# Sparse attention in steps of three instead of two, with transposed keys one trio ahead

## The chip, the cores and the metric

The program runs on one core of a Trainium2 chip. The metric is the device time of one execution in microseconds. Engines are named as in the profile: PE is TensorE's matmul, PEld its weight load, DVE VectorE, ACT ScalarE, POOL GpSimd and SP SyncE, which here only issues transfers.

## The reference

One layer of graph attention and one layer of experts, each with a residual, on 4096 nodes of 512 features. All arithmetic is float32.

```python
def _L0_gnn_ref(x, adj, Wks, Wqs, Wvs, Wo):       # 8 heads of 64
    adj = max(adj, eye)
    q, k, v = (einsum('nd,hdk->hnk', x, W) for W in (Wqs, Wks, Wvs))
    scores = einsum('hqk,hmk->hqm', q, k) * 64 ** -0.5
    scores = scores + 0.01 * eye - 1e16 * (1 - adj)
    return einsum('hqm,hmk,hko->qo', softmax(scores), v, Wo)

def _L0_ffn_ref(x, Wg, bg, W1, b1, W2, b2):       # 8 experts, the best 2 of each row
    w, idx = top_k(x @ Wg + bg, 2)
    y = gelu(x @ W1[e] + b1[e]) @ W2[e] + b2[e]   # for the two chosen e
    return sum(softmax(w) * y)

x = x + _L0_gnn_ref(layernorm(x), adj, ...)
x = x + _L0_ffn_ref(layernorm(x), ...)
```

The adjacency is sparse, with more edges among the first nodes: an edge has a probability that falls with the numbers of both nodes.

## The kernel before

The program has three stages. The first (0 to about 467 us) normalises x, makes keys, values and queries, turns the adjacency into bit masks, and builds for each tile of 128 queries a list of the nodes that some query of the tile is joined to. A row of `kv_d` holds for one node its 512 keys, its values with a column of ones, and its mask words: `KVW` words of four bytes, 4,640 bytes in all. The third stage (from about 1543 us) runs the experts on rows sorted by expert. The stage between, attention, is where the change lies.

**Steps.** Each of the 32 tiles of queries (`i`) is worked through in steps (L639 to L650). The first step of a tile is "own": the 128 nodes of the tile itself. A "both" step has 128 gathered nodes that are scored against all 128 queries. A "split" step has twice 128 gathered nodes, of which one set is scored against the first 64 queries, the other against the last 64. `ROOM` (L31) says how many there are: with `(3, 2, 3)` a tile has own, both, split, both, split, split. There are 270 steps in all, 115 both, 123 split and 32 own, that need 361 gathered sets of 128 rows and 32 of a tile's own.

**Duos.** Up to two consecutive steps of a tile make a duo (L654). The loop L1100 to L1118 has one slot `n` for each duo, and in it, in program order: `scores` of duo n + 1, `values` of duo n, the ends of tiles and new transfers, the jobs that were laid on slot n (`later`), and `turn` of duo n + 3. Engines run their instructions in this order; semaphores tie them where data does.

- `turn` (L711): PE transposes the keys of the step, four or eight 128 x 128 transposes, into a PSUM buffer of `bank`; ACT copies it to `kT` (L720); DVE spreads the mask words to `t` (L730).
- `scores` (L744): PE multiplies kT with the queries, 8 products of 64 x 128 for an own or both step, 32 of 64 x 64 for a split one (L755; each float32 product shows as two matmuls in the trace). ACT takes the exponential into `pr` (L762), DVE multiplies by the mask (L766, L768).
- `values` (L774): PE multiplies pr with the values of the ring's row and adds up in `o` (L783).

**Buffers.** `ps_r` has three PSUM buffers of two banks each; `bank()` (L661) hands them out in turn for scores, transposes and all jobs. `ps_o` has the last two banks. In SBUF, `step` has four buffers of kT, four of pr and six of t. `ring` is one large tile of 24 rows (`RING`); each row takes one gather.

**Transfers.** `issue` (L1053) puts the gathers of duos up to n + 5 (`AHEAD`) into the queues. A gather (L691) is an indirect DMA issued by POOL; a tile's own rows and its queries come through SP. A gather waits until the values of the step that held its row 24 rows earlier are done. When all gathers are issued, `load_weights` (L1075) brings the experts' weights into parts of the ring that fall free: `PARTS` = 7 of the eight parts lie over the ring, the eighth goes to memory that is freed when attention ends (L1116).

**Ends of tiles.** After a tile's last duo, `end_of` (L798) divides by the sums and lays jobs on later slots: transposing (`flip_o`, n + 1), the projection with Wo (`project`, L823, n + 2) and the residual. After every fourth tile `route` (L850) lays the routing of four tiles on the slots after: `root`, `norm` (ACT, L885), `flip`, `gate`, `rank`, `place`, `number_places`, `pick`, `weigh`, `finish`, and eight `scatter`s (L1010) that POOL writes with indirect DMAs to `xs_d`, two in each of four slots. The last four tiles are routed as groups of two, one and one.

Of the kernel before, what the change touches and what calls it, by code (L numbers as in the profile page):

```python
# [9 lines left out]
F32 = mybir.dt.float32  # L10
BF16 = mybir.dt.bfloat16
I32 = mybir.dt.int32
U16 = mybir.dt.uint16
# [7 lines left out]
P = 128  # L21
# [54 lines left out]
def _fast(ctx, tc, dram, flag, x, adj, Wks, Wqs, Wvs, Wo, Wg, bg, W1, b1, W2, b2, out):  # L76
    nc = tc.nc
    N, D = x.shape
    H, _, KD = Wks.shape
# [8 lines left out]
    NW = P // 16  # L88
# [231 lines left out]
    with ExitStack() as s1:  # L320
# [198 lines left out]
        def job(n, f, *args):  # L519
            jobs.setdefault(n, []).append(lambda: f(*args))  # L520

        begins = [0]
        for i in range(NT):
            begins.append(begins[-1] + (2 * DC if i < TPB else 3 * DC))
            s = begins[i]
# [7 lines left out]
        for h in range(NHC):  # L533
            s = 5 + 5 * h
# [57 lines left out]
        for i in range(NT):  # L592
            b, t = divmod(i, TPB)
# [28 lines left out]
    xs_ = {}  # L622
    scatters = []

    RING, PARTS = 24, 7
    SW = E * HID
    ringp = ctx.enter_context(tc.tile_pool(name="ring", bufs=1))
    ring = ringp.tile([P, PARTS * SW], I32, name="ring")
    with ExitStack() as s2:
# [3 lines left out]
        mid = s2.enter_context(tc.tile_pool(name="mid", bufs=1, side="right"))  # L633
        s3 = ExitStack()
        qp = s3.enter_context(tc.tile_pool(name="qp", bufs=1))
        step = s3.enter_context(tc.tile_pool(name="step", bufs=4))


        steps = []  # L639
# [11 lines left out]

        duos = []  # L654
        for i in range(NT):
            own = [n for n, st in enumerate(steps) if st["i"] == i]
            duos += [own[k : k + 2] for k in range(0, len(own), 2)]

        S = len(duos)

        def bank(name, shape):  # L661

            t = ps_r.tile([P, 2, 512], F32, tag="r", name=name)
            n = 1
            for k in shape:
                n *= k
            v = t.rearrange("p b f -> p (b f)")[:, :n]
            if len(shape) == 2:
                v = v.rearrange("p (a b) -> p a b", b=shape[1])
            elif len(shape) == 3:  # L670
                v = v.rearrange("p (a b c) -> p a b c", b=shape[1], c=shape[2])
            return v
# [5 lines left out]
        def at(n, job):  # L678
            later.setdefault(n, []).append(job)
# [22 lines left out]
        def load_q(i):  # L702
            qs[i] = qp.tile([P, NP, P], F32, tag="q", bufs=3, name=f"q_{i}")
            nc.sync.dma_start(out=qs[i], in_=q_d[:, :, ts(i, P)])
# [6 lines left out]
        def turn(s):  # L711
            st = steps[s]
            i = st["i"]
            nk = len(st["kv"])
            pk = bank(f"pkT_{s}", [2 * NP, P])
            for x, g in enumerate(st["kv"]):
                for p in range(NP):
                    nc.tensor.transpose(pk[:, x * NP + p, :], g[:, ts(p, P)], ident)  # L718
            kT = step.tile([P, 2 * NP, P], F32, tag="kT", name=f"kT_{s}")
            nc.scalar.copy(kT[:, : nk * NP], pk[:, : nk * NP])  # L720
            st["kT"] = [kT[:, x * NP : (x + 1) * NP] for x in range(nk)]
            t = step.tile([P, NW, 16], U16, tag="t", bufs=6, name=f"t_{s}")
            if st["kind"] == "own":
                words = [own_words[:, i, :]]
            else:
                words = [wv[:, i * NW : (i + 1) * NW] for wv in st["wv"]]
            nw = NW // len(words)
            for x, wv in enumerate(words):
                w = slice(x * nw, (x + 1) * nw)
                nc.vector.tensor_tensor(  # L730
                    t[:, w], wv[:, w].unsqueeze(2).to_broadcast([P, nw, 16]), bits[:, w],
                    op=ALU.bitwise_and,
                )
            st["t"] = t.rearrange("p w k -> p (w k)")
            if st["kind"] == "own":
                m = step.tile([P, P], F32, tag="m", bufs=2, name=f"m_{s}")
                nc.vector.scalar_tensor_tensor(
                    m, st["t"], 0.0, eye, op0=ALU.is_gt, op1=ALU.max
                )
                st["m"] = m  # L740
# [3 lines left out]
        def scores(s):  # L744
            st = steps[s]
            q, parts = qs[st["i"]], st["kT"]
            nq = P // len(parts)
            ps = bank(f"ps_{s}", [2, HD])

            nk = P if len(parts) == 1 else HALF  # L750
            for x, kT in enumerate(parts):
                for p in range(NP):
                    for r in range(2):
                        for c in range(0, P, nk):
                            nc.tensor.matmul(  # L755
                                ps[c : c + nk, r, p * P + x * nq : p * P + (x + 1) * nq],
                                kT[r * KD : (r + 1) * KD, p, c : c + nk],
                                q[r * KD : (r + 1) * KD, p, x * nq : (x + 1) * nq],
                                start=True, stop=True,
                            )  # L760
            pr = step.tile([P, H, P], F32, tag="pr", bufs=4, name=f"pr_{s}")
            nc.scalar.activation(  # L762
                pr.rearrange("p h q -> p (h q)"), ps.rearrange("p r f -> p (r f)"), AF.Exp
            )
            if st["kind"] == "own":
                nc.vector.tensor_mul(pr, pr, st["m"].unsqueeze(1).to_broadcast([P, H, P]))  # L766
            else:
                nc.vector.scalar_tensor_tensor(  # L768
                    pr, st["t"].unsqueeze(1).to_broadcast([P, H, P]), 0.0, pr,
                    op0=ALU.is_gt, op1=ALU.mult,  # L770
                )
            st["pr"] = pr
# [77 lines left out]
        def route(g, n):  # L850
# [159 lines left out]
            def scatter(k, j):  # L1010
                nc.gpsimd.memset(tick, 0.0)
                s = nc.gpsimd.indirect_dma_start(  # L1012
                    out=xs_d,
                    out_offset=bass.IndirectOffsetOnAxis(
                        ap=hold["slot"][:, j, k : k + 1], axis=0
                    ),
                    in_=xs_[m[k]], in_offset=None,
                )
                for t in scatters:
                    tc.declare_no_dep(s.ins, t.ins, reason="other rows")  # L1020
                scatters.append(s)
# [18 lines left out]
            n += 4  # L1040
            for k in range(G):
                for j in range(2):
                    at(n + k, lambda k=k, j=j: scatter(k, j))

        AHEAD = 5
        tick = small.tile([1, 1], F32, bufs=1, name="tick")
        wo = mid.tile([P, NP, D], F32, name="wo")
        nc.scalar.dma_start(
# [2 lines left out]
        issued = 0  # L1051

        def issue(upto, n):  # L1053
            nonlocal issued, rows_
            while issued < min(upto, S):
                sts = [steps[s] for s in duos[issued]]
                need = sum(max(1, len(st["at"])) for st in sts)
                if any(behind[(rows_ + k) % RING] > n for k in range(need)):
                    return
                for s in duos[issued]:  # L1060
                    st = steps[s]
                    if st["k"] == 0:
                        load_q(st["i"])
                    st["to"] = []
                    for x in range(max(1, len(st["at"]))):
                        k = rows_ % RING
                        behind[k] = issued
                        rows_ += 1
                        st["to"].append(ring[:, k * KVW : (k + 1) * KVW])
                        gather(s, x)  # L1070
                issued += 1
# [3 lines left out]
        def load_weights(n):  # L1075

            for k in range(PARTS):
                over_ = range(k * SW // KVW, min(RING, ((k + 1) * SW - 1) // KVW + 1))
                if issued == S and wparts[k] is None and all(behind[r] <= n for r in over_):
                    load_part(k, ring[:, k * SW : (k + 1) * SW].bitcast(F32))  # L1080
# [5 lines left out]
                nc.sync.dma_start(out=v[:, e], in_=from_[e, ts(c, P), :])  # L1086
            wparts[k] = v

        def duo(f, n):
            if n < S:  # L1090
                for s in duos[n]:
                    f(s)

        issue(AHEAD, -1)
        duo(turn, 0)
        duo(turn, 1)
        duo(scores, 0)
        duo(turn, 2)
        n = 0
        while n < S or any(k >= n for k in later):  # L1100
            duo(scores, n + 1)
            duo(values, n)
            if n < S:
                end = steps[duos[n][-1]]
                if end["last"]:
                    end_of(end["i"], n)
                    load_xi(end["i"])
                issue(n + 1 + AHEAD, n)
                load_weights(n)
            for job in later.pop(n, []):  # L1110
                job()
            duo(turn, n + 3)
            if n == S:
                s3.close()
                wff = ctx.enter_context(tc.tile_pool(name="wff", bufs=1))
                for k in range(PARTS, DC + HC):  # L1116
                    load_part(k, wff.tile([P, SW], F32, name=f"w_{k}"))
            n += 1  # L1118
# [730 lines left out]
```

## Time and profile before

| what | us |
|---|---|
| median of 3 runs (2100.89 to 2114.70) | 2109.29 |
| profiled execution | 2102.14 |
| its span, first to last instruction | 2100.4 |
| stretch 467 to 1489 (attention): PE busy | 945.3 of 1022 |
| same stretch: DVE, ACT, POOL busy | 531.5, 524.0, 450.7 |
| stretch 1489 to 1543 (routing ends): PE busy | 19.5 of 54 |

A row of a timeline is start, duration, engine, line, operation, what is written and read, and how often; a bracket tells how long the engine had been idle and what ended that. A row of waits is engine and line, what it waited for, the sum in us, how often and the longest. "issue" stands for idle time in which the engine waited for no semaphore that the profile shows. A matmul's end is modelled in the profile, so distances are taken from start to start.

### The profile page before, as it was taken

What the parts mean: (1) busy time and instruction counts of PE and PEld (TensorE: products, weight loads), DVE (VectorE), ACT (ScalarE), POOL (GpSimd) and SP (SyncE); (2) the same over time, 40 slices, a digit from 0 to 9 for tenths busy, and PEclk for the clock granted to TensorE, in tenths of its full rate; (3) what the DMA queues carried; (4) which work ended last, traced back from release to release, by engine and by line L of the source; (5) the groups of instructions that cost most, each with busy time, mean ns of one, the idle gap of its engine ahead of it and who ended that gap; (6) DMA issues with size and microseconds to landing.
All of it is one profiled execution on the core that took longest, in us unless ns stands there. A gap on an engine that the chain in (4) does not pass through costs nothing. (4 is left out here: it accounts for less than half of the span.)

```text
span 2100.4 us, 59242 instructions
## 1 busy us (share of the span) xinstructions
PE 1953.5 (93%) x25393; PEld 1302.2 (62%) x25393; DVE 952.8 (45%) x2470; ACT 794.9 (38%) x1161; POOL 603.9 (29%) x725
## 2 busy tenths in 40 slices
PE   8899999999998988998989998889579999999996
PEld 4344444448887877877878787778434444444443
DVE  3455556525544554555555554555613232332322
ACT  3233233316554544545545554445212222222221
POOL 2000000025354445354362726341312212222121
PEclk9999999999999999999999999999779999999998
DMA  9877877249787759788595959677834344433432
GB/s 371 261 248 249 260 253 249 81 179 387 239 280 252 261 202 358 237 292 291 194 376 170 366 184 359 222 276 243 306 116 70 68 71 67 70 68 69 70 66 43
DMA packets 181278, 442.30 MB, mean 211 GB/s; under 512 B 28176, under 2 KB 44560, under 8 KB 180880
## 3 DMA queue, kind: packets, MB, share of 16 engines
q0 software_dynamic: 67712, 251.55, 37.7%
q1 hardware_dynamic: 89136, 154.17, 22.7%
q10 hardware_dynamic: 24160, 32.68, 4.4%
q8 instruction: 205, 3.36, 0.6%
q14 instruction: 65, 0.53, 0.1%
HBM read 364.92 MB, written 73.42 MB: 209 GB/s over the span
## 5 line engine op out<-in xcount | busy, mean ns | idle before, releaser
L691 POOL DMA_INDIRECT ring<-kv_d,idx x361 | 396.5, 1098 | 836.6 <-ACT l L298 438.0
L768 DVE SCALAR_TENSOR_TENSOR pr<-t,pr 128x1024 f32<-128x1024 uint16 x238 | 285.1, 1228 | 265.7 <-ACT pr L762 265.7
L755 PE MATMUL ps<-q,kT 64*64 64x64 f32 (+1 forms) x10224 | 306.5, 237 | 27.5 <-issue 19.8
L783 PE MATMUL o<-ring,pr 128*64 128x65 f32 x8640 | 295.0, 225 | 33.2 <-issue 33.0
L720 ACT COPY kT<-pkT 128x512 f32<-128x512 f32 (+1 forms) x270 | 198.6, 783 | 324.6 <-PE pkT L718 315.7
L755 PEld LDWEIGHTS ps<-q,kT 64*64 64x64 f32 (+1 forms) x10224 | 273.0, 148 | 61.9 <-issue 40.6
L783 PEld LDWEIGHTS o<-ring,pr 128*64 128x64 f32 x8640 | 271.7, 139 | 49.3 <-issue 33.6
L762 ACT ACTIVATE pr<-ps 128x1024 f32<-128x1024 f32 x270 | 270.9, 1026 | 58.2 <-PE ps L755 53.3
L1227 PE MATMUL ph<-ring,xT 128*128 x552 | 251.6, 599 | 0.7 <-ACT xT L1217 0.7
L1265 POOL DMA_INDIRECT out_dram<-y,r x69 | 107.4, 1557 | 448.6 <-ACT y L1264 443.9
L718 PE MATMUL pkT<-ident,ring 128*128 128x128 f32 x1572 | 204.6, 279 | 13.4 <-ACT kT L720 6.5
L718 PEld LDWEIGHTS pkT<-ident,ring 128*128 128x128 f32 x1572 | 176.5, 143 | 39.3 <-issue 26.9
L1251 PE MATMUL py_e<-ring,hT 128*128 x414 | 189.2, 593 | 1.6 <-ACT hT L1245 1.6
L1227 PEld LDWEIGHTS ph<-ring,xT 128*128 128x128 f32 x552 | 100.6, 192 | 101.8 <-issue 100.1
L1264 ACT ACTIVATE y<-y,wt 128x512 f32<-128x512 f32 x69 | 49.8, 721 | 246.3 <-DVE y L1263 246.3
L1232 DVE COPY h<-ph 128x512 f32<-128x512 f32 x69 | 47.7, 692 | 200.7 <-PE ph L1227 200.7
L1263 DVE TENSOR_TENSOR y<-py_e,bb 128x512 f32<-128x512 f32 x69 | 47.7, 692 | 194.5 <-PE py_e L1251 194.5
L599 PE MATMUL pv<-wv,xT 128*128 128x512 f32 x256 | 132.5, 613 | 0.0
L599 PE MATMUL pk<-wk,xT 128*128 128x512 f32 x256 | 128.9, 615 | 0.7 <-ACT xT L394 0.7
L584 PE MATMUL pq<-xT,wq 128*128 128x512 f32 x256 | 125.9, 607 | 0.0
L1012 POOL DMA_INDIRECT xs_d<-x,slot_i x64 | 69.4, 1085 | 195.0 <-DVE t L730 89.2
L823 PE MATMUL py<-wo,oT 128*128 128x512 f32 x256 | 122.6, 623 | 0.0
(257 smaller groups left out, 1833.6 us busy)
## 6 DMA issues: line engine op xcount, KB each, us to landing
adj<-in_adj_dram SPq DMA_DIRECT2D x64, 1024.0 KB, 5.7
r<-xs_d SPq DMA_DIRECT2D x69, 258.0 KB, 2.7
kv_d<-kvr ACTq DMA_DIRECT2D x32, 516.0 KB, 5.8
ring<-kv_d SPq DMA_DIRECT2D x32, 516.0 KB, 6.8
ring<-in_L_ffn_W_dram SPq DMA_DIRECT2D x56, 256.0 KB, 5.3
xt<-in_x_dram SPq DMA_DIRECT2D x32, 256.0 KB, 6.1
q_d<-qT ACTq DMA_DIRECT2D x32, 256.0 KB, 2.7
q<-q_d SPq DMA_DIRECT2D x32, 256.0 KB, 5.6
```

The lines of the kernel that those rows point to most:

```text
L584: nc.tensor.matmul(pq, w["q"][:, c, ts(p, P)], xTs[b][:, c, :], start=(c == 0), stop=(c == DC - 1),)
L599: nc.tensor.matmul(pk, xTs[b][:, c, ts(t, P)], w[n][:, c, :], start=(c == 0), stop=(c == DC - 1),)
L691: nc.gpsimd.indirect_dma_start(out=g, out_offset=None, in_=kv_d, in_offset=bass.IndirectOffsetOnAxis(ap=idx[i // GL][:, i % GL, a : a + 1] ...
L718: nc.tensor.transpose(pk[:, x * NP + p, :], g[:, ts(p, P)], ident)
L720: nc.scalar.copy(kT[:, : nk * NP], pk[:, : nk * NP])
L755: nc.tensor.matmul(ps[c : c + nk, r, p * P + x * nq : p * P + (x + 1) * nq], kT[r * KD : (r + 1) * KD, p, c : c + nk], q[r * KD : (r + 1) ...
L762: nc.scalar.activation(pr.rearrange("p h q -> p (h q)"), ps.rearrange("p r f -> p (r f)"), AF.Exp)
L768: nc.vector.scalar_tensor_tensor(pr, st["t"].unsqueeze(1).to_broadcast([P, H, P]), 0.0, pr, op0=ALU.is_gt, op1=ALU.mult,)
L783: nc.tensor.matmul(o[c * HALF : (c + 1) * HALF, h // NP, (h % NP) * VW : (h % NP + 1) * VW], pr[:, hd * NP + p, c * HALF : (c + 1) * HALF] ...
L823: nc.tensor.matmul(hold["py"], hold["oT"][:, c, :], wo[:, c, :], start=(c == 0), stop=(c == NP - 1),)
L1227: nc.tensor.matmul(ph, xTs[b][:, c, :], wparts[c][:, bass.ds(es[b], 1), :], start=(c == 0), stop=(c == DC - 1),)
L1251: nc.tensor.matmul(py, hTs[b][:, c, :], wparts[DC + c][:, bass.ds(es[b], 1), :], start=(c == 0), stop=(c == HC - 1),)
```

## The change

Three consecutive steps of a tile make a trio; the loop has one slot for each trio. In a slot the order is `scores` of trio n + 1, `turn` of trio n + 2, `values` of trio n, then ends, transfers and jobs. So keys are transposed one trio ahead of their scores, ahead of the values and of the jobs. The ring has 21 rows and lies over six of the eight weight parts; gathers are issued up to three trios ahead. Buffers: kT three (was four), pr six (was four), t eight (was six). A group's eight scatters are laid four in each of two slots.

```diff
-    RING, PARTS = 24, 7
+    RING, PARTS = 21, 6
...
-        step = s3.enter_context(tc.tile_pool(name="step", bufs=4))
+        step = s3.enter_context(tc.tile_pool(name="step", bufs=3))
...
-        duos = []
+        trios = []
         for i in range(NT):
             own = [n for n, st in enumerate(steps) if st["i"] == i]
-            duos += [own[k : k + 2] for k in range(0, len(own), 2)]
-
-        S = len(duos)
+            trios += [own[k : k + 3] for k in range(0, len(own), 3)]
+
+        S = len(trios)
...
-            t = step.tile([P, NW, 16], U16, tag="t", bufs=6, name=f"t_{s}")
+            t = step.tile([P, NW, 16], U16, tag="t", bufs=8, name=f"t_{s}")
...
-            pr = step.tile([P, H, P], F32, tag="pr", bufs=4, name=f"pr_{s}")
+            pr = step.tile([P, H, P], F32, tag="pr", bufs=6, name=f"pr_{s}")
...
             for k in range(G):
                 for j in range(2):
-                    at(n + k, lambda k=k, j=j: scatter(k, j))
-
-        AHEAD = 5
+                    at(n + k // 2, lambda k=k, j=j: scatter(k, j))
+
+        AHEAD = 3
...
         issue(AHEAD, -1)
-        duo(turn, 0)
-        duo(turn, 1)
-        duo(scores, 0)
-        duo(turn, 2)
+        trio(turn, 0)
+        trio(scores, 0)
+        trio(turn, 1)
         n = 0
         while n < S or any(k >= n for k in later):
-            duo(scores, n + 1)
-            duo(values, n)
+            trio(scores, n + 1)
+            trio(turn, n + 2)
+            trio(values, n)
             if n < S:
-                end = steps[duos[n][-1]]
+                end = steps[trios[n][-1]]
...
             for job in later.pop(n, []):
                 job()
-            duo(turn, n + 3)
```

The helper `duo`, which calls a function for each step of a duo, becomes `trio`; `issue` reads `trios` in place of `duos`.

More of the change, by code (lines that the diff above doesn't have):

```diff
@@ L1055, in issue @@
             while issued < min(upto, S):
-                sts = [steps[s] for s in duos[issued]]
+                sts = [steps[s] for s in trios[issued]]
                 need = sum(max(1, len(st["at"])) for st in sts)
@@ L1059, in issue @@
                     return
-                for s in duos[issued]:
+                for s in trios[issued]:
                     st = steps[s]
@@ L1087, in load_part, with trio @@
             wparts[k] = v
-        def duo(f, n):
+        def trio(f, n):
             if n < S:
-                for s in duos[n]:
+                for s in trios[n]:
                     f(s)
         issue(AHEAD, -1)
-        duo(turn, 0)
-        duo(turn, 1)
-        duo(scores, 0)
-        duo(turn, 2)
+        trio(turn, 0)
+        trio(scores, 0)
+        trio(turn, 1)
         n = 0
         while n < S or any(k >= n for k in later):
-            duo(scores, n + 1)
-            duo(values, n)
+            trio(scores, n + 1)
+            trio(turn, n + 2)
+            trio(values, n)
             if n < S:
-                end = steps[duos[n][-1]]
+                end = steps[trios[n][-1]]
                 if end["last"]:
```

## The prediction

> **What bounds the kernel now.** I read the page's slices first, then busy time by stage, then PE's waits, then the timelines. The attention loop runs from the first transposed key at 466 us to about 1489 us. Before it lie the projections, after it 54 us of routing and the experts; the change touches only the loop and its two ends.
>
> ```profile
> PE 1953.5 (93%) x25393; PEld 1302.2 (62%) x25393; DVE 952.8 (45%) x2470; ACT 794.9 (38%) x1161; POOL 603.9 (29%) x725
> ...
> PE   8899999999998988998989998889579999999996
> ...
> DMA  9877877249787759788595959677834344433432
> ```
> ```profile
> 467.00:1489.00 1022.00, 945.34 (x21166) 817.41 (x21163) 531.50 (x1257) 524.01 (x639) 450.68 (x483) 0.98 0.78 275
> 1489.00:1543.00 54.00, 19.50 (x97) 14.85 (x98) 24.98 (x154) 5.36 (x10) 22.25 (x44) 0.66 0.73 275
> ```
>
> The columns are span, then busy PE, PEld, DVE, ACT, POOL, clock, DMA share, GB/s. In the loop PE is busy 945 of 1022 us; DVE and ACT are only half busy. PE is the bound, with 77 us idle. What ends the idle time:
>
> ```profile
> PE o L783 <- issue: 33.0, 22, 3.1
> PE ps L755 <- issue: 19.8, 15, 3.3
> ...
> PE ps L755 <- ACT oT L817: 3.4, 5, 1.9
> ...
> PE ps L755 <- DVE place L949: 2.8, 3, 1.4
> PE pkT L718 <- DMA ring<-kv_d,idx: 2.7, 1, 2.7
> PE ps L755 <- ACT kT L720: 1.1, 3, 0.6
> PE pkT L718 <- ACT kT L720: 1.0, 1, 1.0
> ```
>
> Waits for another engine or a gather come to only some 12 us; the rest is "issue". Those pauses stand at multiples of 127 or 128 matmuls (I numbered PE's matmuls in the trace: 4526 and 4654, 5670, 5798, 5926, 6053), each about 2.3 us after a 16,384-byte packet of the instruction queue starts. They are instruction supply, some 58 us, and no semaphore of the program. Now the rhythm:
>
> ```profile
> 1151.23 2.06 PE L755 MATMUL ps<-q,kT 64*128 64x128 f32 x32
> 1153.21 1.16 PE L783 MATMUL o<-ring,pr 128*64 128x65 f32 x32
> 1154.30 1.53 PE L718 MATMUL pkT<-ident,ring 128*128 128x128 f32 x12
> 1155.76 2.29 PE L755 MATMUL ps<-q,kT 64*64 64x64 f32 x80
> 1157.97 2.09 PE L783 MATMUL o<-ring,pr 128*64 128x65 f32 x64
> 1159.99 0.66 PE L815 MATMUL po<-ident,on 128*128 128x128 f32 x4
> 1160.49 1.04 PE L718 MATMUL pkT<-ident,ring 128*128 128x128 f32 x8
> ```
> ```profile
> 1156.99 2.13 ACT L762 ACTIVATE pr<-ps 128x1024 f32<-128x1024 f32 x2
> 1160.69 0.58 ACT L817 COPY oT<-po 128x512 f32<-128x512 f32 x1 [1.57 <-PE po L815]
> ```
> ```profile
>   PE o L783: 203.6, 72
>   DVE pr L768: 98.9, 36
> ```
>
> Scores, values and transposes follow one another with no gap. The last two lines are what POOL's gathers (L691) waited for: ring rows, not the other way round. So before, transfers come early and PE sets the pace.
>
> **What the skill says.** "Runtime: NRT & Kernel Launch", section "Instruction fetch mechanics": instructions come in 16 KiB blocks of 256, fetched by the sequencer's own queue. The 128 matmul and weight-load pairs between pauses agree; that this is "mostly hidden" does not hold here (58 us). "Perfetto Trace Analysis", "Matmuls": rotate PSUM banks so that evacuation of one lies under the next group's matmuls. The trace agrees: ACT's copies and exponentials end few PE waits. "DMA: Bandwidth & Descriptors", "Anatomy of one DMA": about 2.0 us plus bytes / 436e3. A gather of 128 rows of 4,640 bytes would take an estimated 3.4 us; the packets of the software queue, taken 128 to a gather, give 3.9 us at least and 7.7 us in the median from issue to the last packet, so I use the measured ones.
>
> **Part 1: fewer changes of kind on PE.** Per row of a table the distances above give the price of starting a group. Values: 32 matmuls take 1.09, 64 take 2.02 us: 0.94 a step and 0.15 a group. Transposes (least distances over the loop: 0.97, 1.40 and 1.84 us for 8, 12, 16): 0.109 each and 0.10 a group. Scores: 16 full ones take 1.09, 32 take 1.98: about 0.18 for each run of one shape. By ROOM, 270 steps make 144 duos and 101 trios, and runs of one shape in the scores go from 208 to 203. Gain: 43 x (0.15 + 0.10) + 5 x 0.18 = 11.7, say **-12 us**. Nothing hides it: PE is the bound.
>
> **Part 2: instruction supply.** The number of blocks stays. A block hurts where its 128 matmuls run fast: 17 ns each in split scores, 29 in values, 109 in transposes. Before, scores and values stand together and the transposes after; now transposes stand between them. I took the durations above block by block: a twentieth of the blocks stays under 3 us, and the quarter that lay under 4.1 us now lies under 4.5. If a block needed 4.5 us to arrive, 9 us would come back, at 5.5 us some 8. The fetch itself is not told by the trace in full, so bounds -14 and +8; I take **-5 us**.
>
> **Part 3: waits that go.** The oT and place waits came from a bank of a job just ahead of two transposes and a score; now scores of up to three steps lie between. Of 12 us perhaps half: **-5 us**, bounds 0 and -11.
>
> **Part 4: a new wait on PSUM.** bank() turns through three buffers. The order is now scores a, b, c, transposes a, b, c, so transposes c take the buffer of scores c, whose exponential has only transposes a and b to hide behind. From the ACT lines: exponential starts 0.14 us after its scores end, takes 1.02, and PE goes on 0.05 later: 1.21 us. Transposes a and b of an "own, both" start hold two rows: 2 x 0.436 = 0.87, leaving 0.34 us. With a split among them it is 1.31 and the wait is gone. 31 tiles after the first begin with own and both, tile 0 has six trios of both alone: 37 x 0.34 = **+12 us**. If it hit every trio, 101 x 0.34 = 34. Behind the waiting transposes stand values, whose operands have long been ready; that is why it costs.
>
> **Part 5: routing on ACT.** In one slot of each of seven groups of four tiles ACT has two copies of x2T and two normalisations (0.58 and 0.81 us each) ahead of three exponentials. These used to have values of two steps and jobs to hide behind. Exponential a starts some 1.0 us late: 7 x about 0.7, **+5 us**, bounds 0 and 10.
>
> **Part 6: the gathers.** The ring loses three rows of 24, and three trios (12 to 13 rows) are held where three duos (8) were, so 8 rows instead of 16 are in flight. Summing PE work from the values that free a row to the transposes that need it: median 37 us before (the trace has 42 from issue, pauses included), now 25, least 12 to 17. Against it: a burst of four or five rows at 1.25 us of POOL each, and 4.3 to 8 us to land: 9 to 14 us. Usually that fits. It is tight where four scatters (1.3 us each with the memset) stand in POOL's queue in each of two slots: those after them in the queue, two trios of gathers, have 0 to 5 us left. SP's own rows, q and x keep their order and some 12 us. I take **+4 us**, bounds 0 and +40.
>
> **Part 7: both ends.** The first trios need gathers at about 477 and 484 us, when the before trace lands them: +1 at most. After the last values, POOL now has eight scatters of the last group of four tiles (10.5 us) that ran beside the loop; POOL had 13.75 us idle there. Two weight parts instead of one follow at the end, 4 MB, some 13 us at the 321 GB/s seen there, and the first expert starts 54 us after the loop. **+1 us**, bounds 0 and +8.
>
> Six pr and eight t buffers cost nothing: pr of a trio is written after the values two trios back. kT's three are read before they are rewritten.
>
> Sum: -12 - 5 - 5 + 12 + 5 + 4 + 1 = 0. The profiled execution took 2102.14 us (span 2100.4), so it stays at 2102; the median of the runs is 7 us above it at 2109.29. I predict **2108 us**.
>
> **Rivals.**
> - *The gathers fall behind* (slower). POOL's order and the smaller ring decide: once a trio's last row lands after scores n+1 end, every us is PE's, since transposes now stand ahead of values. It decides from a landing time of about 12 us or scatters that wait longer than one slot. For it: DMA is 0.78 busy, and where the trace before has scatters among gathers, slack fell from 32 to 6 us. Against: the margins of part 6. At 5 us for each of seven groups' two trios less what part 6 has, plus some single rows: 7 x 6 = 42 less 4, about 2146.
> - *The PSUM wait at every trio* (slower, mildly): part 4 at 34 instead of 12: 2130. For it: ACT may be late by jobs. Against: the three-row case is hidden by 0.1 us.
> - *Instruction supply improves more* (faster). If the burst of scores and values was what emptied it, half of 58 us goes, and part 5 is hidden: -24 - 5, about 2079. Against: scores of a split and two boths are as fast as before.
> - *PE is unmoved in substance*: this is the forecast, gains and losses of a dozen us each.
>
> **Numbers.** A measurement of this kernel tells about 1% (21 us) from no change. Forecast 0.60, gathers late 0.18, PSUM at every trio 0.08, supply 0.14. The range takes the gains alone (-31, to 2078) nearly in full and the gathers' case: 2080 to 2150. The likeliest case alone: 2092 to 2125. Faster by over 1%: 0.14; slower: 0.18 plus half of 0.08, 0.22; within: 0.64.
>
> **What would show it.** Right: L718 and L783 in about 101 groups each; PE in the loop 12 to 17 us less for the same work; new waits of some 0.3 us of pkT L718 on ACT pr L762, about 40; "issue" of PE at 45 to 60 us. POOL's wait for o L783 shorter in lead: gathers no longer 37 to 42 us ahead of use but some 25. Wrong: pkT L718 waiting for DMA ring<-kv_d more than 10 us in all (gathers), more than 25 us on pr (PSUM), "issue" under 35 us (supply), or a stretch after the loop longer than 62 us.

## The result, and the profile after

The kernel after takes 2092.86 us (median of 10 runs, 2089.51 to 2099.88), the kernel before 2106.02 (10 runs, 2097.95 to 2114.70). The ratio is 0.995, with a 95% interval of 0.9933 to 0.9966: 7 to 14 us less, within the 1% that I called no change. The profiled execution took 2096.47 us (span 2094.7).

The page, the same lines as before (busy time of each engine, then PE and DMA in 40 slices):

```profile
PE 1954.8 (93%) x25393; PEld 1295.5 (62%) x25393; DVE 953.3 (46%) x2470; ACT 791.4 (38%) x1161; POOL 565.9 (27%) x725
...
PE   8899999999999999898999999999579999999996
...
DMA  9877877248688878777778687978933334443432
```

As many matmuls and weight loads, and nearly the same busy time. The same two stretches by stage (span, then busy PE, PEld, DVE, ACT, POOL, clock, DMA share, GB/s):

```profile
467.00:1489.00 1022.00, 950.30 (x21188) 813.41 (x21187) 533.98 (x1262) 520.97 (x641) 409.55 (x478) 0.98 0.79 275
1489.00:1543.00 54.00, 19.76 (x83) 14.58 (x82) 23.50 (x148) 5.34 (x11) 25.21 (x48) 0.63 0.78 284
```

These windows are fixed, and the loop now ends sooner: from the first transposed key to the end of the last values it took 1022.4 us before (466.4 to 1488.8) and takes 1011.6 now (466.6 to 1478.2). From there to the first expert's work it is 54.1 and 59.8 us. What PE waited for:

```profile
PE o L783 <- issue: 27.0, 24, 2.4
PE ps L755 <- issue: 26.6, 24, 2.7
...
PE ps L755 <- ACT kT L720: 5.3, 1, 5.3
...
PE pkT L718 <- ACT kT L720: 2.5, 2, 1.8
...
PE pkT L718 <- issue: 1.7, 2, 1.0
PE pkT L718 <- ACT pr L762: 1.5, 5, 0.7
...
PE pkT L718 <- DMA ring<-kv_d: 1.3, 2, 0.9
```

The waits for oT (3.4 us), place (2.8) and the one gather (2.7) that the list of before had are gone or nearly so. "issue" is still the bulk. The new PSUM wait is hardly in this list, because the list counts PE's idle time alone, from the modelled end of the last matmul, and the wait shows at the weight loads. The view of one line, L718, of what matmul and weight load there each sat idle until (us in all, times), has both:

```profile
  ACT pr L762: 14.6, 40
  issue: 7.1, 7
  ACT kT L720: 3.5, 3
  DMA ring<-kv_d: 1.3, 2
```

The weight loads alone waited 35 times for the exponential, 13.1 us in all; five of these waits show at the matmul too, and the 40 counts them twice. From start to start, the 35 transposes came 10.5 us later than the usual 109 ns after the one before. This is what one of the longer waits looks like, in the timeline of PE, with the exponential of the third scores and the weight load from the same window:

```profile
1120.54 1.16 PE L755 MATMUL ps<-q,kT 64*64 64x64 f32 x64
1121.64 1.10 PE L718 MATMUL pkT<-ident,ring 128*128 128x128 f32 x8
1122.95 1.09 PE L718 MATMUL pkT<-ident,ring 128*128 128x128 f32 x8 [0.22 <-ACT pr L762]
1123.98 3.24 PE L783 MATMUL o<-ring,pr 128*64 128x65 f32 x96
```
```profile
1121.88 1.02 ACT L762 ACTIVATE pr<-ps 128x1024 f32<-128x1024 f32 x1 [0.64 <-PE ps L755]
```
```profile
1122.95 0.85 PEld L718 LDWEIGHTS pkT<-ident,ring 128*128 128x128 f32 x8 [0.46 <-ACT pr L762]
```

The exponential ends at 1122.90 and the second group of transposes starts at 1122.95. That it is PSUM and not data shows in what waits: the transposes read only the ring, and what they need from `pr`'s exponential is the buffer that it empties. The 96 values in one run show the trio. POOL's gathers (L691) waited for this (over the whole span, so "issue" has the first stage in it):

```profile
  issue: 491.0, 183
  PE o L783: 240.4, 62
```

Gathers still wait for ring rows, and PE never waited for a gather. From issue to the transposes that use them it is 26.6 us in the median (37.5 before) and 13.3 at least.

**Where the time went.** I added up PE's start-to-start times by what is written, between the same two events, without the idle time, and the idle time by its cause:

| us | before | after |
|---|---|---|
| scores `ps` | 296.6 | 296.3 |
| values `o` | 285.4 | 280.3 |
| transposes `pkT`, about 9 us of the new wait in it | 195.5 | 200.5 |
| projection `py`, 3.5 us of it moved behind the loop | 112.3 | 108.8 |
| other PE work | 56.4 | 58.3 |
| idle, "issue" | 58.3 | 54.6 |
| idle, all other causes | 17.9 | 12.8 |
| loop | 1022.4 | 1011.6 |

The loop wins 10.8 us and the stretch after it loses 5.7, so the two profiled executions differ by 5.7 us in span, while the medians differ by 13. The rest is scatter of single executions: that of before lies 3.9 us under its median, that of after 3.6 over it.

**The granted clock** is not the same in the two. In the profiled loops it stood at half for 41.0 us before and 30.7 after. A values matmul started 30.6 ns after the last one at full clock and 54.5 at half (before), so 10.3 us less at half clock are worth an estimated 4.5 us. The timed runs tell the same: in 77 runs of the kernel before, on three chips, a mean clock lower by 0.001 went with some 2 us more, and the median clock was 0.974 in these and 0.976 in the ten runs of the kernel after. So an estimated 4 of the 13 us go with the clock. The variants below moved it too (median 0.972 in e2, 0.968 in e5, 0.979 in e7); whether the order of the work brings this is open. It is not the whole gain: e3 below wins the same 10.8 us of the loop with 41.0 us at half clock, as many as before.

### The profile page after: what moved, and what is told of

Its sections match the earlier page's. It is cut to its first block, busy times and chain, and to the rows that moved or that the text cites. A ratio compares the mean times of both kernels' runs of the same rounds, so it can differ in the third digit from the quotient of the medians.

```text
span 2094.7 us, 59190 instructions
## 1 busy us (share of the span) xinstructions
PE 1954.8 (93%) x25393; PEld 1295.5 (62%) x25393; DVE 953.3 (46%) x2470; ACT 791.4 (38%) x1161; POOL 565.9 (27%) x725
## 5 line engine op out<-in xcount | busy, mean ns | idle before, releaser
L691 POOL DMA_INDIRECT ring<-kv_d,idx x361 | 355.9, 986 | 963.0 <-issue 491.0
L755 PE MATMUL ps<-q,kT 64*64 64x64 f32 (+1 forms) x10224 | 303.2, 237 | 33.5 <-issue 26.6
L783 PE MATMUL o<-ring,pr 128*64 128x65 f32 x8640 | 287.3, 225 | 27.0 <-issue 27.0
L718 PE MATMUL pkT<-ident,ring 128*128 128x128 f32 x1572 | 204.3, 279 | 10.3 <-ACT kT L720 2.5
L718 PEld LDWEIGHTS pkT<-ident,ring 128*128 128x128 f32 x1572 | 171.2, 142 | 28.7 <-ACT pr L762 13.1
L1250 PE MATMUL py_e<-ring,hT 128*128 x276 | 130.0, 593 | 1.6 <-ACT hT L1244 1.6
L1250 PE MATMUL py_e<-w,hT 128*128 x276 | 129.7, 592 | 0.0
```

The source lines that it names most:

```text
L691: nc.gpsimd.indirect_dma_start(out=g, out_offset=None, in_=kv_d, in_offset=bass.IndirectOffsetOnAxis(ap=idx[i // GL][:, i % GL, a : a + 1] ...
L755: nc.tensor.matmul(ps[c : c + nk, r, p * P + x * nq : p * P + (x + 1) * nq], kT[r * KD : (r + 1) * KD, p, c : c + nk], q[r * KD : (r + 1) ...
L783: nc.tensor.matmul(o[c * HALF : (c + 1) * HALF, h // NP, (h % NP) * VW : (h % NP + 1) * VW], pr[:, hd * NP + p, c * HALF : (c + 1) * HALF] ...
L1250: nc.tensor.matmul(py, hTs[b][:, c, :], wparts[DC + c][:, bass.ds(es[b], 1), :], start=(c == 0), stop=(c == HC - 1),)
```

## The experiments

Two things were open. First, "no change" was a sum of gains and losses that cancel: is each one there, or is nothing there? Second, the largest term of idle time, some 55 us of "issue", hardly moved: is it instruction supply, and what sets it? My theory was that the terms are there at about their forecast size: PSUM costs what L718 shows (P), starts of groups and of shapes have their price (G), and "issue" is supply, set by how fast PE uses up its blocks (S). The main rival to P and G was that the order of the three stages, not the grouping, makes the gain (O). Diffs are against the kernel after unless it is said otherwise. Ratios are always to the kernel before, timed on the same chip. "Loop" and "issue" are sums as in the table above.

**The PSUM wait (e1).** The transposes of a trio begin with its split steps, which take 16 transposes instead of 8.

```diff
+        def turns(n):
+            if n < S:
+                for s in sorted(trios[n], key=lambda s: steps[s]["kind"] != "split"):
+                    turn(s)
...
-            trio(turn, n + 2)
+            turns(n + 2)
```

> The trio kernel with one edit: within a trio the split step is transposed first. Nothing else moves. Theory P (new waits of transposes on the exponentials cost about 14 us of PE in the loop): in an own-both-split trio three rows of transposes instead of two now hide the exponential, so the sum of pkT waiting for pr falls from 14.6 us to under 5 us and the time falls 8 to 11 us below the trio kernel, to about 0.990 of before. Rival R (the wait is slack, PE would be held by something else, such as instruction supply): the waits go but 'issue' grows by as much, and the time stays at 0.995.

Measured: 2086.52 us, 0.9914 [0.9885, 0.9942]. The view of L718:

```profile
  issue: 9.0, 9
  ACT pr L762: 2.0, 6
```

The wait falls from 14.6 us in this view (13.1 at 35 weight loads) to 2.0 (6 of them); transposes from 200.5 to 191.7 us; loop 1002.4, "issue" 56.8. So the wait is real, and its cause is the length of what stands ahead of it. The gain, 7 to 8 us by the ratios, is just under the 8 to 11 that I expected. The same edit run again (e11), with the runs of the last part:

> The trio kernel with the split transposed first, once more, to stand beside the next kernel on one chip. Where the kernel before takes 2105 us: 0.991. On a chip that itself interrupts dense stretches of PE (the kernel before at 2260 us): the gain may be gone, 0.995 to 1.02, since fewer pauses make PE denser.

2085.66 us, 0.9914 [0.9887, 0.9942]. Both intervals reach 0.0009 into that of the kernel after; that the ratio came twice, and the trace, speak for the gain.

**Grouping without the order (e2).** Trios as they are, but values ahead of transposes. This is not quite the old order: the kernel before transposes duo n + 3, behind the jobs and so one duo earlier, and e2 transposes trio n + 2, ahead of the jobs. The old lead with trios would need six buffers of kT and was not run.

```diff
             trio(scores, n + 1)
-            trio(turn, n + 2)
             trio(values, n)
+            trio(turn, n + 2)
```

> The trio kernel with values ahead of transposes in each slot (scores n+1, values n, transposes n+2, ends and jobs). Still 101 slots, so the gain of fewer group starts stays. Theory P: the waits of pkT on pr go (14.6 us to near 0), but scores of the next trio now stand right behind transposes, so new waits of ps on kT appear after trios of one step, estimated 13 x 0.5 = 7 us: 3 to 8 us below the trio kernel, 0.991 to 0.994. Theory S (instruction supply gains from transposes between scores and values): 'issue' of PE in the loop grows from 55 to about 60 us again and takes 4 to 5 us of that back. Rival: if order alone made the gain, time goes back to 1.000.

Measured: 2102.15 us, 0.9986 [0.9969, 1.0002]. This missed: trios in this order bring nothing that can be told from zero. PE's waits:

```profile
PE o L783 <- issue: 54.5, 32, 3.9
PE ps L755 <- ACT kT L720: 14.8, 16, 5.4
PE ps L755 <- issue: 12.2, 10, 3.1
PE pkT L718 <- issue: 11.4, 11, 2.0
```

Fewer group starts did bring what I had forecast for them: PE's work for scores, values and transposes is 764.6 us in the loop, 12.9 less than before. But "issue" is 77.3 us, 19 more than before, and scores now wait for the copy of kT that was made just ahead of them (waits for kT are 16.8 us in the loop, 7.6 before). Three scores and three values, 17 and 29 ns a matmul, follow one another with nothing slow between.

**The order without grouping (e3).** Against the kernel before: duos, ring of 24 rows, AHEAD 5 and four scatter slots kept, but transposes of duo n + 2 between scores and values.

```diff
-        duo(turn, 1)
         duo(scores, 0)
-        duo(turn, 2)
+        duo(turn, 1)
...
             duo(scores, n + 1)
+            duo(turn, n + 2)
             duo(values, n)
...
-            duo(turn, n + 3)
```

> The kernel before with duos kept, and only the order changed: scores n+1, transposes n+2, values n, ends, jobs. Ring, AHEAD and buffers as before. Theory G (the gain comes from 43 fewer slots, 11 to 12 us of group starts): this keeps 144 slots, so only the supply part is left, 'issue' down by 4 to 5 us, and no PSUM wait since transposes b take the buffer of scores a: 0.997 to 0.999. Rival O (order is what gained): as fast as the trio kernel or faster, 0.993 to 0.995.

Measured: 2089.58 us, 0.9935 [0.9911, 0.996]. The gain is the rival's size, not mine.

```profile
PE ps L755 <- issue: 24.6, 18, 3.9
PE o L783 <- issue: 21.5, 19, 3.2
...
PE ps L755 <- ACT kT L720: 6.9, 2, 6.3
```

"issue" is 47.4 us in the loop, 11 less than before, and all other idle time there 8.1 instead of 17.9. PE's work for scores, values and transposes takes 7.1 us of this back. So the order, and not the three steps at once, is the part that brings the gain. The sums of the profiled loops, in us, beside the ratios of the timed runs:

| steps and order | ratio | "issue" | other idle | `ps`, `o`, `pkT` |
|---|---|---|---|---|
| before: duos; scores, values, transposes (one duo earlier) | 1 | 58.3 | 17.9 | 777.5 |
| e3: duos; scores, transposes, values | 0.9935 | 47.4 | 8.1 | 784.6 |
| e2: trios; scores, values, transposes | 0.9986 | 77.3 | 18.6 | 764.6 |
| after: trios; scores, transposes, values | 0.9950 | 54.6 | 12.8 | 777.1, with 9.0 of the new wait |
| e1: the same, split transposes first | 0.9914 | 56.8 | 8.0 | 770.2 |

In either order trios make PE's work 13 to 17 us shorter and "issue" 7 to 19 us longer.

**The smaller ring (e4).** Against the kernel before.

```diff
-    RING, PARTS = 24, 7
+    RING, PARTS = 21, 6
...
-        AHEAD = 5
+        AHEAD = 4
```

> The kernel before with the trio kernel's ring alone: 21 rows over six weight parts, gathers up to four duos ahead (rather than 24, seven, five). Theory G: gathers come with room to spare, the lead from issue to use falls from 42 to some 33 us, no new wait of pkT on the ring: 0.999 to 1.001. Rival D (a smaller ring or later weights cost something that the trio kernel also pays, so its gain on PE is larger than 10 us): 1.002 to 1.006, with waits of pkT on ring or a longer stretch after the loop.

Measured: 2102.78 us, 0.9991 [0.9972, 1.001]. Three rows and one duo of lead cost nothing that can be measured in time. The trace, taken in one of the variant's slowest executions (2112.1 us), does show some of the waits that rival D named: transposes waited 6.8 us (3 times) for a tile's own rows, which SP brings, and the least time from a gather's landing to its use was 1.0 us (4.2 before).

**Runs of one shape (e5).** The steps of a tile in the order own, boths, splits, so that shapes alternate less.

```diff
-            for k in range(max(tm, ta)):
-                if k < tm:
-                    order.append(("both", (ta + k,)))
-                if k < ta:
-                    order.append(("split", (k, ta + tm + k)))
+            for k in range(tm):
+                order.append(("both", (ta + k,)))
+            for k in range(ta):
+                order.append(("split", (k, ta + tm + k)))
```

> The trio kernel with the steps of a tile ordered own, boths, splits instead of both and split in turn. Runs of one shape in the scores fall from 203 to 118. Theory G (starts of groups are what counts, 0.18 us each): 85 x 0.18 = 15 us faster, 0.988. Theory S (instruction supply: 256 instructions to a block, a pause where a block is used up in under some 4.5 us): three splits in a row use 192 matmuls in 3.1 us, so 'issue' of PE in the loop grows from 55 to some 90 us and eats the gain and more: 1.000 to 1.010.

Measured: 2133.89 us, 1.0127 [1.0102, 1.0152]. Runs of one shape in the scores fall from 203 to 118, and scores take 11 us less (284.9; 85 starts at 0.18 would be 15). It costs far more:

```profile
PE ps L754 <- issue: 56.9, 29, 4.5
PE o L782 <- issue: 31.4, 22, 2.9
```

"issue" is 95.8 us, where theory S had said some 90. Long runs of split scores use instructions up fastest, and that is where PE stops.

**Fewer matmuls for the same work (e6, e7, e8).** If "issue" is supply, it must go when the same time holds fewer instructions, though nothing in waits or buffers changes. e6 makes the values of an own or both step as one product of 128 columns instead of two of 64; e7 takes all 128 keys of a split set in one product against its 64 queries, instead of two of 64 keys; e8 is e1 with both.

```diff
-                for c in range(2):
+                w = P // len(kv)
+                for c in range(len(kv)):
...
-                        o[c * HALF : (c + 1) * HALF, ...
-                        pr[:, hd * NP + p, c * HALF : (c + 1) * HALF],
+                        o[c * w : (c + 1) * w, ...
+                        pr[:, hd * NP + p, c * w : (c + 1) * w],
```
```diff
-            nk = P if len(parts) == 1 else HALF
+            nk = P
```

> The trio kernel with one edit: in own and both steps a head's values are one product of 128 columns of weights in place of two of 64. That leaves 147 x 16 = 2352 of 21,168 matmuls of the loop out and, by the estimate that a product of 65 columns on the whole array takes as long as two halves side by side (0.94 us a step now), no time of PE. Theory S: fewer and slower-used blocks, 'issue' in the loop from 55 to 30 to 40 us: 0.986 to 0.990. Rival (pauses are not of supply, or halves side by side are really faster): 0.995 or slower, up to 147 x 0.9 = 130 us slower if the halves run fully side by side.

> The trio kernel with one edit: in split steps a product of scores takes all 128 keys in place of two of 64. That leaves 123 x 32 = 3936 matmuls of the loop out, the densest ones (17 ns each). Theory S: 'issue' from 55 to 20 to 30 us, PE's busy time as before (16 full ones take 0.90 us, 64 quarter ones 0.93): 0.980 to 0.986. Rival (pauses not of supply, or 64 columns do not fill a pass and cost twice): no gain or up to 123 x 0.9 = 110 us slower.

> Both edits, and within a trio the split transposed first. Theory S with theory P: 'issue' below 15 us, waits of pkT on pr below 4 us: 0.965 to 0.975. If the two whole forms cost PE time, the sum of what they cost apart.

Measured: e6 2172.35 us, 1.0315 [1.0274, 1.0356]; e7 2102.81, 0.9988 [0.9976, 1.0]; e8 2221.43, 1.0558 [1.0529, 1.0586]. In e7 the stretch of the loop and PE's waits for "issue" (the latter from a list of the loop alone):

```profile
467.00:1489.00 1022.00, 1009.08 (x17202) 894.57 (x17201) 531.88 (x1219) 519.29 (x636) 404.55 (x477) 0.98 0.78 270
```
```profile
PE ps L755 <- issue: 0.7, 1, 0.7
...
PE pkT L718 <- issue: 0.7, 1, 0.7
```

With 17,202 matmuls in place of 21,188, "issue" falls from 54.6 to 1.0 us in the loop. The traces have a second sign that it is supply: each of the 43 pauses of "issue" in the loop before, and of the 49 after, ends 1.2 to 1.7 us after a 16,384-byte packet of the instruction queue has ended, and all stand within 12 instructions of one place in a count of 256. But all three runs missed in time: that wider products cost PE nothing was wrong. In e7 scores cost 78 us more (374.3), 0.63 for each of 123 split steps, so nothing is won; values took 11 us less (269.4), which no edit explains. In e6 "issue" falls to 16.9, and values rise from 280.3 to 403.1 us. In e8 "issue" is gone, and the two prices add up (values 400.2, scores 377.3). The groups of values by shape show the price of one (line, what is written and read, shape, count, busy us, mean ns of one):

```profile
L784 PE MATMUL o<-ring,pr 128*128 128x65 f32 x2352 | 280.3, 276 | 0.0
...
L784 PE MATMUL o<-ring,pr 128*64 128x65 f32 x3936 | 138.6, 225 | 0.8 <-issue 0.8
```

By busy time and count, a whole product takes 119 ns of PE and a half 35, though one lasts 276 and 225 ns: products overlap, the halves more. The 122.8 us more, over 147 own and both steps, are 0.84 us a step on top of 0.94.

**Whole scores in a few steps (e9, e10, e12).** The rest of the idea: whole scores only where a split step follows a split step, 22 of 123 in trios. e9 is e1 with it, e10 is e3 with it for 21 duos.

```diff
+        wide = {
+            b for m in trios for a, b in zip(m, m[1:])
+            if steps[a]["kind"] == steps[b]["kind"] == "split"
+        }
...
-            nk = P if len(parts) == 1 else HALF
+            nk = P if len(parts) == 1 or s in wide else HALF
```

> The trio kernel with the split transposed first, and with whole products of scores (128 keys, half as many matmuls) only in a split that follows a split in its trio: 22 of 123. Theory S: whole products cost 0.63 us a step (measured over all 123: 78 us), 14 us here, and take the fastest blocks away; by the same count of blocks as explains the pauses of the other orders, 'issue' of PE falls from 57 to about 30 us: 10 us below the kernel with the split first alone, 0.986 to 0.990 of before. Rival (pauses move to the next block rather than go): 'issue' stays over 45 us and the time is 0.992 or slower.

> Duos with transposes between scores and values, and whole products in the second split of the 21 duos of two splits. Theory S: 'issue' from 47 to about 25 us for 13 us of PE: 0.987 to 0.991. If duos and trios then differ by no more than 0.003, what threes gain over twos in group starts (12 us) is smaller than what order and pauses move.

Measured: e9 2317.97 us, 1.0242 [1.0206, 1.0279]; e10 2359.21, 1.0439 [1.0404, 1.0474]. Both missed, and both ran on a chip on which the kernel before itself took 2260.91 us. PE was stopped there in another way, and since neither e1 nor e3 was run on that chip, the two say nothing of whole scores as such. A stretch of e9's timeline on PE:

```profile
916.83 0.35 PE L759 MATMUL ps<-q,kT 64*64 64x64 f32 x6 [0.41 <-issue]
917.56 0.35 PE L759 MATMUL ps<-q,kT 64*64 64x64 f32 x4 [0.38 <-issue]
...
919.02 0.49 PE L759 MATMUL ps<-q,kT 64*64 64x64 f32 x4 [1.10 <-issue]
919.76 0.26 PE L759 MATMUL ps<-q,kT 64*64 64x64 f32 x1 [0.25 <-issue]
```

"issue" was 114.9 us in 239 pauses, and only some 7 us of that at the borders of blocks of 256 instructions, where all but 2 us of it lies in each kernel on the other chips. The clock was granted at half for 215 us of e9's loop besides, by the price above an estimated 94 us lost. e9 was run again elsewhere, as e12; e10 was not:

> The trio kernel with the split transposed first and whole products of scores in 22 splits, once more. Theory S on a chip where the kernel before takes 2105 us: 0.986 to 0.990, 'issue' near 30 us, below the kernel run beside it. Rival (pauses move): 0.992 or slower. On a chip that interrupts dense stretches: slower than the kernel beside it if denser work is what brings the interruptions, since it has the fewest pauses of supply.

Measured: 2073.48 us (2069.76 to 2082.21), 0.9856 [0.983, 0.9882], where the kernel before took 2105.2. This is the best version, by the two ratios about 0.9% below the kernel after. Its waits, over the whole span:

```profile
PE ps L759 <- issue: 15.2, 15, 2.3
PE o L787 <- issue: 12.7, 14, 2.1
...
PE pkT L722 <- issue: 5.7, 5, 2.2
```

"issue" falls from e1's 56.8 to 33.6 us, and scores rise by some 21 (317.8): 2 us gained on paper, loop 998.5 in place of 1002.4. Its profiled execution was its slowest, so the profile understates it; the timed difference to e11 on the same chip is 12 us, of which the traces show 3, so most of this gain is measured and not explained.

## Why the prediction was right, point by point

I forecast 2108 us with gains and losses that cancel. The time is 2092.86, 15 us under the forecast, inside its range and on its side of 1%. That is less than it sounds: I forecast practically no change, the runs show a gain of 13 us that is clear of noise, and a range of 70 us held both. The sum was 0 against the profiled execution; the profiled executions differ by -5.7 us, and the terms are these:

| part | predicted | measured | from |
|---|---|---|---|
| 1 group starts | -12 | -9.4 | `o` -5.1, `ps` -0.3, `pkT` without its wait -4.0 |
| 2 supply | -5 | -3.7 | "issue" 58.3 to 54.6 |
| 3 waits that go | -5 | -8.5 | oT 3.4 to 0.4, place 2.8 and the gather 2.7 to 0 |
| 4 PSUM wait | +12 | +10.5 | L718 on pr, 35 times, from start to start |
| 5 routing on ACT | +5 | +0.5 | x2T 1.3 to 1.8 |
| 6 gathers | +4 | +1.3 | a tile's own rows, by SP |
| 7 ends | +1 | +1.2 | 5.7 behind the loop, 4.5 of it work that left the loop |

These sum to -8.1; other PE work (+1.9) and kT (+0.3) make it -5.9.

*Part 1* was right in its mechanism, but its net was luck in part. The profile has 101 groups each of transposes and values (143 and 144 before). Grouping alone is worth what I said: -12.9 us in e2. But the order costs starts of its own, +7.1 in e3, which I had at nothing, and an estimated 4.5 of the 9.4 us go with the clock. Nor is the table exact to a few us: one kernel run twice, e1 and e11, differs by 5.4 us in `o` and by 2.3 in `ps`, `o` and `pkT` together.

*Part 2* was right in its sum only, and that was luck. I took the order and the grouping as one change of block times. They are two, of opposite sign: grouping adds 19 us of "issue" with values ahead of transposes (e2), and the order takes 11 off duos (e3) and 23 off trios (77.3 to 54.6). Had I worked each by itself, I would have seen that the supply gives back most of what part 1 wins. That a block used up in under about 4.5 us ends in a pause was a good assumption: it gave 90 us of "issue" for e5 ahead of the run, and 95.8 came. I took PE's blocks of 256 instructions and the time from a block's first matmul to the next one's, pauses left out. The sum of 5.0 us less this time, where positive, is 62, 54, 73, 51 and 94 us for before, after, e2, e3 and e5; the traces have 58, 55, 77, 47 and 96. The 5.0 is fitted to these five, and e6 (36, trace 17) and e12 (23, trace 34) come out worse, so it ranks the orders and is no exact law. The section "Instruction fetch mechanics" of the Trainium skill's "Runtime: NRT & Kernel Launch" gives the block of 256 that this rests on; its "mostly hidden" does not hold here, with 58.3 us of pauses at the borders before and 1.0 in e7. Why a block takes that long is not shown.

*Part 3* went further than half, and not for the whole of my reason. I put it down to scores of three steps, but in e3, with scores of two, the waits for oT and place are 0 and 0.3 us as well. So the order does it: transposes no longer stand between the jobs and the next scores. The gather's wait was a single one.

*Part 4* is the step that carried the forecast: 35 waits that cost 0.30 us each, predicted 37 of 0.34. It came from reading the order of three buffers and one line of ACT. e1 shows that it was also the one loss that could be had back, for 2 us more of "issue": 0.995 becomes 0.9914.

*Part 5* was over-sized by 4.5 us. I reckoned with an exponential that starts 1.0 us late in seven slots. In the trace, exponentials start more than 0.6 us after their scores in three slots, by 0.94 us at most. That transposes between scores and values cover the rest is likely and not shown.

*Part 6* was over-sized too, though the lead was about as forecast: 26.6 us, and 25 predicted. The 42 and 7.7 us that the prediction takes for medians of the trace are upper quartiles; the medians are 37.5 us from issue to use and 5.8 from issue to landing, and 26.6 and 5.5 after. The least slack from landing to use is 4.4 us, 4.2 before: the tight cases were no tighter. In e4 a ring of 21 rows and a shorter lead cost duos no measurable time either, but its waits for own rows (6.8 us) show that the term is not nothing.

*Part 7* was right. Beyond the 4.5 us of PE work moved behind the loop, the first expert comes 1.2 us later.

*The rivals.* Late gathers: no wait of PE for a gather by POOL. PSUM at every trio: 35 of 101. Supply improves more: not in this kernel, but e12 shows that 23 us of it could be had, for 21 us of scores. That the profile says 5.7 where the runs say 13 was in the nature of one execution each. Of the 15 us that the forecast was too high, 3 are the kernel before, which came to 2106.02 in ten runs after 2109.29 in three; parts 5 and 6 make 7.

Left open: the trio with the old ring, buffers and scatter slots was not run, so the ring is known to be free only in duos (e4), and the rest only by the waits. And e3 and e1 differ by 0.0021 with overlapping intervals, so whether trios are worth anything over duos once the order is changed is not settled.

## What to carry to other kernels

When a change does two things, price each alone and run each alone: here grouping saved group starts and lost them to the supply, the order saved supply and waits and cost some starts, and the sum hid that. Where PE is the bound and stalls for "issue" at a steady count of instructions, look at how fast each block of 256 is used up; put slow instructions between fast ones, and try a few wider matmuls where the fast ones are densest (0.9856 on one chip; on another the same kernel lost). Before moving a stage in a program order, walk the buffer rotation through the new order: what now takes the buffer of whom, and is that one's reader still hidden?

## What the runs showed of the hardware

- PE's pauses stand at the borders of 256 instructions (matmuls, weight loads and semaphore instructions together), and each of them, before and after, ends 1.2 to 1.7 us after a 16,384-byte packet of the instruction queue has ended. Of blocks used up in under 3.5 us most end in a pause (before 11 of 16, after 7 of 11, e5 24 of 28); of those over 6.5 us practically none (0 of 54, 2 of 43, 0 of 51).
- Products with 64 columns of weights cost PE less than half of one with 128: 32 of them take 0.94 us a step, where 16 of 128 columns take 0.84 more (e6). For scores the difference is 0.63 us a step (e7). The halves are twice the instructions, so the faster form is also the one that empties the supply.
- One chip stopped PE inside dense runs of scores, with pauses of mostly 0.25 to 0.5 us that no semaphore and no block border explains. Of the 114.9 us of pauses in e9's loop, 90 lie in stretches of half clock or in the 5 us before one, together 29% of the loop; half clock took 215 us of it, and 31 us of the same kernel's loop in e12. The granted clock was 0.947 in the median there for the kernel before, 0.974 on the others, and the kernel before took 2260.91 instead of some 2105 us. The kernel with whole scores in some steps lost more there (e9 1.0242, e12 0.9856). The cause is not settled.
